# Attention and a 7x7 depthwise convolution with group norms: the second norm's statistics on ScalarE, attention steps in groups of eight, and half a convolution tile moved to VectorE

## Chip, cores and metric

The kernel runs on one core of a Trainium2 chip. The metric is device time in microseconds (us). TensorE (PE) multiplies matrices, VectorE (DVE), ScalarE (ACT) and GpSimd (POOL) work on rows of 128 partitions, and SyncE (SP) issues transfers. Every engine takes its instructions in the order in which the program lists them, and transfers are issued by SP, by GpSimd and, at the very end, by ScalarE.

## The reference

x has 16 images of 384 channels and 32 x 32 pixels, in float32. Both layers begin with a group norm over 32 groups of 12 channels (no learned scale), and both add their result to their input:

```python
x = x + attention(gn(x))     # 8 heads of 48 channels, 1x1 convolutions for q,k,v and for the output, a bias
x = x + depthwise(gn(x), w)  # 7x7, padding 3; w is the mean of the weight and its three rotations

def gn(v):                   # per image and group of 12 channels
    return (v - mean(v)) / sqrt(var(v) + 1e-5)
def attention(h):            # n = 1024 pixels are the tokens
    q, k, v = split(w_qkv @ h)
    return w_proj @ (softmax(q @ k.T / sqrt(48)) @ v) + b_proj
```

Below, x1 is the sum after the first layer: it is the input of the second norm, and the convolution is added to it.

## The kernel before

**Layout.** Channels lie on the partitions, in three tiles of 128 channels by 1024 pixels per image. The four rotations make the 49 weights of a channel, wsym. The attention of an image is cut into four units, one for each pair of heads; a unit has 16 steps, two halves of the queries by eight tiles of 128 keys. The S part of a step (L425) multiplies k with q for both heads of the pair into a PSUM tile of 128 x 1024, and ScalarE takes the exponential of it (L433). The AV part (L441) multiplies the exponentials with v and adds up over the eight key tiles; a column of ones in v gives the sum of the exponentials. After eight AV parts ScalarE copies the result, o, to SBUF (L452). The maximum is not subtracted; a check at the end repeats everything by another path if a sum was out of range.

**One image on TensorE.** S and AV parts are issued in groups: first the S parts of a group, then other work, then its AV parts, then other work. The sizes of the groups are a list:

```python
SIZES = [7] * 8 + [8]        # 64 steps of an image
```

The other work is the q,k projection of the next image in six chunks (`qk_step`, L374, evacuated at L381), the v projection in four (`v_step`, L400, L409) and the output projection in three (`proj_step`, L492). Three PSUM tiles of 128 x 1024 (ps_s) serve S and all of this in turn, and two of 128 x 512 (ps_o) serve AV.

**From o to the output projection.** `finish` sends the row of sums out and back through DRAM (two rows out, one transfer back, all by SP) so that they lie on 128 partitions; `finish2` (`invert`) takes the reciprocal on VectorE and sends it out and back, spread over 64 partitions a head; `finish3` (`divide`) multiplies. For the last unit of an image six rows of o are then copied by SP into the three packed tiles that the projection reads. `project` follows: three times a projection, evacuated on ScalarE with the bias added, and x added to the result by an accumulating transfer that GpSimd issues. The six rows that complete the packed q,k tiles (`qk_rest`) go through SP too.

**The norms.** The class `Stats` has the steps of one norm: `channels` (L230: BATCH_NORM_STATS2 on VectorE, twice a tile), `gather` (two transfers by GpSimd that bring the 12 channels of a group together), `groups` (aggregate and an inverse square root of about 14 small VectorE operations, then two transfers to spread the scales to the channels) and `apply` (L296: one ScalarE operation a tile). For the first and the last image `groups_on_pe` averages over groups with small matmuls instead. The statistics of x for images 2 to 15 are taken once, early: 42 tiles stream in (`stream_in`, `stream_stats`), `stream_groups` computes all scales, and seven transfers bring them to the tile x_sc through DRAM (gr_all, L363). `begin_x` loads x of the next image once v of the current one is done, and queues its apply.

**The convolution.** VectorE does it by taps (`conv_tap`, L549): x1 += w * shifted xn, one operation for each of the 49 offsets and each tile, up to three tiles in turn. Four of the 48 tiles (channel tiles 2 and 1 of images 14 and 15, PE_TILES) are done by TensorE instead, in pieces (`conv_on_pe`, L651; halves h = 0 and 1 of the rows, two parts each), with shifted copies of xn (sh, `conv_load`) that come from DRAM; VectorE adds the result at the end (L664). The tile (15, 0), LONE, is summed in two accumulators (`tap_of_two`), which are added at L804.

**The order.** It is written out by the program itself, which keeps two model clocks, `clock` for TensorE and `vclock` for VectorE (US_STEP 1.716 us a step, US_TURN 0.353 a group, and so on). `after(wait, cost, f)` puts a VectorE operation on a heap, due at a model time. `catch_up` issues due operations and, between them, taps, until vclock has reached clock. `applies` is a queue of ScalarE work with due times; its head is issued behind the S parts of a group. `other` issues the other work of TensorE: a due output projection, or chunks.

**The end.** In the first and the last image `fast_finish` and `fast_end` take the place of `finish` and `project`: the sums of the last unit are added up on TensorE (`divide_at_once`), the output projection is done in parts (`proj_part`), and the norm is grouped on TensorE. Behind that the loop issues TensorE's last convolution pieces, and taps beside them, until nothing is left.

## Time and profile before

| what | value |
|---|---|
| median of 3 runs | 2978.39 us (2976.01 to 2980.45) |
| profiled execution | 2982.38 us, its span 2980.2 us |
| granted TensorE clock, mean | 0.996 |
| busy: PE, DVE, ACT, POOL | 2943.7, 2626.3, 1326.4, 200.7 us |
| PE: S, AV, q,k, v, output projections, convolution | 918.4, 910.7, 509.9, 254.6, 220.0, 96.1 us |
| DVE: taps (L549), 2132 of them | 2328.0 us |
| ACT: exponentials (L433), 1024 of them | 954.4 us |
| transfers | 171.27 MB |

The median is over executions that were not profiled; the profiled execution gives all other rows. Its span is what the profile covers, and 2.2 us of its time lie outside the span. The busy time of an engine is the sum over its instructions; the groups of the page add it up by program line, and a row names the output and the inputs with their shapes. Timelines give the start and the length of runs of instructions in us from the start of the span.

### The profile page before, as it was taken

Reading aid. Unit: us, or ns where it says so; the run is one execution under the profiler, and the core shown is the slowest. Engines: PE = TensorE matmul, PEld = TensorE weight load, DVE = VectorE, ACT = ScalarE, POOL = GpSimd, SP = SyncE. Lnnn points to the kernel's source line nnn. Section 1 sums busy time; section 2 is a strip of 40 time slices with the busy share of each in tenths; the row PEclk is TensorE's granted clock in tenths of the full one; section 3 lists DMA queues with packets and bytes.
Section 4 is the critical chain, followed back from the end, with each engine's and each line's share of the span. In section 5 each row is a group of like instructions: output and inputs, shape, how many; then the busy total and the mean of one; then the engine's idle time right before and its main releaser. Section 6 shows DMA issues by size and latency. Waiting matters only on the chain.

```text
span 2980.2 us, 30719 instructions
## 1 busy us (share of the span) xinstructions
PE 2943.7 (99%) x11702; PEld 1191.2 (40%) x11702; DVE 2626.3 (88%) x2771; ACT 1326.4 (45%) x1509; POOL 200.7 (7%) x304
## 2 busy tenths in 40 slices
PE   7999999999999999999999999999999999999998
PEld 4334343343434334343433434343343433434333
DVE  0545983999999999999999999999999999999985
ACT  2533445435354544535454453544445454444600
POOL 0211300000000000000010000001000000100000
PEclk9999999999999999999999999999999999999999
DMA  2641121121312203121120312213031221312424
GB/s 74 241 135 34 24 73 30 26 63 37 66 37 53 51 15 67 43 59 45 31 72 15 67 37 54 56 26 77 16 67 37 52 51 26 67 32 45 119 74 105
DMA packets 73101, 171.27 MB, mean 57 GB/s; under 512 B 30208, under 2 KB 32624, under 8 KB 71408
## 3 DMA queue, kind: packets, MB, share of 16 engines
q0 software_dynamic: 29760, 97.89, 12.1%
q1 hardware_dynamic: 41104, 67.06, 9.9%
q10 hardware_dynamic: 2080, 4.26, 0.6%
q8 instruction: 94, 1.54, 0.2%
q14 instruction: 63, 0.52, 0.1%
HBM read 121.61 MB, written 29.46 MB: 51 GB/s over the span
## 4 chain that ended last, share of the span: by engine, by line
PE 76%; issue 11%; DMA 1%; DVE 1%; POOL 0%; ACT 0%; SPq 0%; POOLq 0%; DVEq 0%
PE ps_s L425 24%; PE acc L441 24%; PE ps_qk L374 14%; PE ps_v L400 7%; PE ps_proj L492 6%; PE ps_conv L651 1%; DVE x L549 1%; DMA x<-in_x 0%; DMA out<-x 0%; DMA sh<-xd 0%; DVE bs_x L230 0%; DMA x_sc<-gr_all 0%; DMA gr_x<-af_x 0%; DVE sum L549 0%; POOL out L559 0%
## 5 line engine op out<-in xcount | busy, mean ns | idle before, releaser
L549 DVE SCALAR_TENSOR_TENSOR x<-xn,wsym,x 128x960 f32<-128x960 f32 (+9 forms) x2132 | 2328.0, 1166 | 49.0 <-ACT xn L296 47.5
L433 ACT ACTIVATE e<-ps_s 128x1024 f32<-128x1024 f32 x1024 | 954.4, 1048 | 357.1 <-PE ps_s L425 353.4
L425 PE MATMUL ps_s<-qk 48*128 48x512 f32 x4096 | 918.4, 597 | 0.0
L441 PE MATMUL acc<-e,v 128*64 128x512 f32 x4096 | 910.7, 596 | 0.0
L425 PEld LDWEIGHTS ps_s<-qk 48*128 48x128 f32 x4096 | 380.0, 185 | 534.4 <-issue 240.6
L441 PEld LDWEIGHTS acc<-e,v 128*64 128x64 f32 x4096 | 281.1, 137 | 608.5 <-issue 600.5
L374 PE MATMUL ps_qk<-x,wqk 128*128 128x512 f32 x1152 | 509.9, 599 | 6.1 <-ACT x L296 3.7
L374 PEld LDWEIGHTS ps_qk<-x,wqk 128*128 128x128 f32 x1152 | 216.4, 191 | 297.2 <-issue 266.4
L381 ACT COPY qk<-ps_qk 128x1024 f32<-128x1024 f32 x96 | 97.2, 1012 | 444.1 <-PE ps_qk L374 444.1
L400 PE MATMUL ps_v<-wv,x 128*128 128x384 f32 x768 | 254.6, 492 | 0.0
L452 ACT COPY o<-acc 128x512 f32<-128x512 f32 x128 | 76.0, 594 | 337.9 <-PE acc L441 337.9
L492 PE MATMUL ps_proj<-o,wp 128*128 128x512 f32 x504 | 220.0, 595 | 0.0
L400 PEld LDWEIGHTS ps_v<-wv,x 128*128 128x128 f32 x768 | 146.0, 192 | 110.3 <-ACT e L433 11.4
L492 PEld LDWEIGHTS ps_proj<-o,wp 128*128 128x128 f32 x504 | 94.6, 190 | 124.5 <-issue 111.2
L409 ACT COPY v<-ps_v 128x384 f32<-128x384 f32 x128 | 55.1, 483 | 187.8 <-PE ps_v L400 187.8
L153 POOL DMA_DIRECT2D x<-in_x x45 | 24.0, 539 | 1536.7 <-ACT v L409 1535.2
L319 DVE BATCH_NORM_STATS2 bs_all<-xs 128x6 f32<-128x512 f32 x84 | 52.5, 680 | 83.8 <-DMA xs<-in_x 83.7
L500 ACT ACTIVATE x<-ps_proj,bp 128x1024 f32<-128x1024 f32 x42 | 46.8, 1113 | 167.7 <-PE ps_proj L492 159.7
L230 DVE BATCH_NORM_STATS2 bs_x<-x 128x6 f32<-128x512 f32 x108 | 69.0, 684 | 50.5 <-DMA x<-in_x 40.9
L477 DVE TENSOR_TENSOR o<-o,inv 128x1024 f32<-128x1024 f32 x62 | 75.5, 1217 | 33.0 <-DMA inv<-inv 22.6
L651 PE MATMUL ps_conv<-sh,mat 128*32 128x480 f32 (+3 forms) x896 | 96.1, 587 | 2.5 <-DMA sh<-xd 2.5
L501 POOL DMA_DIRECT2D x<-in_x x42 | 36.5, 870 | 468.7 <-ACT x L500 463.6
(92 smaller groups left out, 516.1 us busy)
## 6 DMA issues: line engine op xcount, KB each, us to landing
x<-in_x POOLq DMA_DIRECT2D x93, 512.0 KB, 5.4
inv<-inv SPq DMA_DIRECT2D x124, 256.0 KB
out<-x POOLq DMA_DIRECT2D x48, 512.0 KB, 3.7
xs<-in_x POOLq DMA_DIRECT2D x42, 512.0 KB, 6.1
qk<-qk SPq DMA_DIRECT2D x96, 128.0 KB
sh<-xd SPq DMA_DIRECT2D x38, 160.0 KB
o<-o SPq DMA_DIRECT2D x84, 64.0 KB
sh<-xd ACTq DMA_DIRECT2D x26, 160.0 KB
```

Source lines behind the costliest of these rows:

```text
L230: nc.vector.bn_stats(self.bs[:, k, 6 * h : 6 * h + 6], src[:, h * HALF : (h + 1) * HALF])
L374: nc.tensor.matmul(ps[:, h, :], lhsT=wqk[:, k, s, t, :], rhs=xns[b][:, k, h * HALF : (h + 1) * HALF], start=(k == 0), stop=(k == NK - 1),)
L381: nc.scalar.copy(halves(qks[u][:, s, :]), ps)
L400: nc.tensor.matmul(ps[:, j, 0:C], lhsT=xns[b][:, k, t * P : (t + 1) * P], rhs=wv[:, k, :], start=(k == 0), stop=(k == NK - 1),)
L425: nc.tensor.matmul(ps[:, j, :], lhsT=qks[u][r, 1, i * P : (i + 1) * P], rhs=qks[u][r, 0, h * HALF : (h + 1) * HALF], start=True, stop=True,)
L433: nc.scalar.activation(es[n], ps, AF.Exp, scale=SCALE)
L441: nc.tensor.matmul(accs[u, h][64 * j : 64 * j + 64, :], lhsT=v_of(u, i, j), rhs=e[:, j, :], start=(i == 0), stop=(i == NT - 1),)
L452: nc.scalar.copy(os_[u][:, h * HALF : (h + 1) * HALF], accs.pop((u, h)))
L477: nc.vector.tensor_tensor(os_[u], os_[u], invs.pop(u), ALU.mult)
L492: nc.tensor.matmul(ps[:, h, :], lhsT=wp[:, t, o * P : (o + 1) * P], rhs=os_[NP * b + t][:, h * HALF : (h + 1) * HALF], start=(t == 0), sto ...
L549: nc.vector.scalar_tensor_tensor(acc, xn1s[b, k].rearrange("p (h w) -> p h w", w=W)[:, iy, ix], wsym[:, k, dy + PAD, dx + PAD : dx + PAD + 1],
L651: nc.tensor.matmul(pss[b, k][CH * i : CH * (i + 1), h, :].rearrange("p (y x) -> p y x", x=W)[:, :, ox], lhsT=mats[k][:, i, d0 * KS + dx + ...
```

## The change

The change has five parts.

- **Groups.** An image has eight groups of eight steps. Thresholds that name a step of the image (r) are set to multiples of eight.
- **Statistics of x1, images 1 to 12.** The evacuation of the output projection on ScalarE also accumulates its sum over the pixels (`psums`); with the mean of x, kept from the statistics of x (`x_mean`), that gives the mean of x1 (`x1_means`, one VectorE operation). Three squares on ScalarE, with accumulated outputs, give the variances (`square`). The layout is that of the bn statistics, with one entry of six numbers a channel in place of two, so that `gather_x1` moves half as much and VectorE aggregates in one operation. The inverse square root is ln, exp and a product on ScalarE (`groups_x1`). Images 13 and 14 keep VectorE's statistics.
- **Places.** ScalarE's queue `applies` now holds a cost for each entry, and `act_slot(free)` issues entries, behind the S parts of a group or ahead of a q,k chunk, as long as they fit into the time given. The apply of the next image's x goes between the first two and the third output projection (`pending`), or behind the S parts of a group in the images after 0 and 15. For the last unit of an image the waits of `finish` are 6 and 5.5 us instead of 9 and 9.5, and the projection is due 7 us after the division, not 8.
- **Half a tile.** Of the tile (14, 1), SHARED, TensorE does the lower half of the rows only (h = 1); the taps of the upper half go to VectorE. TensorE has 14 pieces of convolution at the end in place of 16.
- **The end.** Taps are issued between the steps of `fast_finish` and `groups_on_pe`, VectorE's model clock gets 4 us behind `fast_finish` in place of 3, and the lone tile takes turns with the others.

The diff, cut to its core:

```diff
 xns, x1s, qks, os_, accs, es, xn1s = {}, {}, {}, {}, {}, {}, {}
-xds, shs, pss, mats = {}, {}, {}, {}
+xds, shs, pss, mats, psums = {}, {}, {}, {}, {}
...
 PE_TILES = [(b, k) for b in (B - 2, B - 1) for k in PE_K]
+SHARED = None if general else (B - 2, PE_K[1])
...
         inverse_sigma(af.unsqueeze(1), mv[:, 0:1], mv[:, 1:2], self.name)
+        self.spread(af)
+    def spread(self, af):
...
         )
-    def groups_on_pe(self, masks):
+    def square(self, src, k):
+        t = tpool.tile([P, N], F32, tag="t", name=f"sq_{self.name}_{k}")
+        nc.scalar.activation(
+            t, src, AF.Square, bias=self.bs[:, k, 1:2], accum_out=self.bs[:, k, 2:3]
+        )
+    def gather_x1(self):
+        ch_d = ddram.tile([C, 6], F32, tag="ch1", name=f"ch_{self.name}")
+        nc.gpsimd.dma_start(ch_d.rearrange("(k p) s -> p k s", p=P), self.bs)
+        self.gs = small.tile([GROUPS, PER * 6], F32, tag="gs1", name=f"gs_{self.name}")
+        nc.gpsimd.dma_start(self.gs, ch_d.rearrange("(g e) s -> g (e s)", e=PER))
+    def aggregate(self):
+        self.mv = small.tile([GROUPS, 2], F32, tag="mv", name=f"mv_{self.name}")
+        nc.vector.bn_aggr(self.mv, self.gs)
+    def groups_x1(self):
+        af = small.tile([GROUPS, 2], F32, tag="af", name=f"af_{self.name}")
+        ln = small.tile([GROUPS, 1], F32, tag="ln", name=f"ln_{self.name}")
+        nc.scalar.activation(ln, self.mv[:, 1:2], AF.Ln, bias=eps[0:GROUPS])
+        nc.scalar.activation(af[:, 0:1], ln, AF.Exp, scale=-0.5)
+        nc.scalar.activation(
+            af[:, 1:2], self.mv[:, 0:1], AF.Identity, scale=af[:, 0:1]
+        )
+        self.spread(af)
+    def groups_on_pe(self, masks, between=lambda: None):
...
         average(0, mean)
+        between()
...
         average(NK, d)
+        between()
...
         )
+def means_of(bs, dst):
+    nc.vector.tensor_reduce(dst, bs[..., 1::3], AX.X, ALU.add)
+    nc.vector.tensor_scalar(dst, dst, -0.25, None, ALU.mult)
...
     M = B - 2
+    means_of(many["bs"], x_mean[:, 2:, :])
...
 def proj_step(b, o):
     ps = psum(f"ps_proj_{b}_{o}")
+    if o == 0:
+        psums[b] = small.tile([P, NK], F32, tag="psums", name=f"psums_{b}")
...
     x1s[b, o] = rpool.tile([P, N], F32, tag="x1", name=f"x1_{b}_{o}")
-    nc.scalar.activation(halves(x1s[b, o]), ps, AF.Identity, bias=bp[:, o : o + 1])
+    nc.scalar.activation(
+        halves(x1s[b, o]),
+        ps,
+        AF.Identity,
+        bias=bp[:, o : o + 1],
+        accum_out=psums[b][:, o : o + 1],
+    )
...
 def conv_tap(b, k, dy, dx, dst=None):
     (oy, iy), (ox, ix) = region(dy, dx)
+    if (b, k) == SHARED:
+        oy = slice(oy.start, min(oy.stop, H // 2))
+        iy = slice(iy.start, oy.stop - oy.start + iy.start)
...
 def conv_end(b, k):
+    if (b, k) == SHARED and not late.get("shared"):
+        late["shared"] = True
+        return
...
 def conv_on_pe(b, k, h, part):
-    if (h, part) == (0, 0):
+    if (b, k) not in pss:
...
 def conv_on_pe_end(b, k):
-    nc.vector.tensor_tensor(
-        halves(x1s[b, k]), pss.pop((b, k)), halves(x1s[b, k]), ALU.add
-    )
+    h = slice((b, k) == SHARED, 2)
+    dst = halves(x1s[b, k])[:, h]
+    nc.vector.tensor_tensor(dst, pss.pop((b, k))[:, h], dst, ALU.add)
...
 NS = U * 2 * NT
-SIZES = [7] * 8 + [8]
+SIZES = [8] * 8
...
 def us_tap(dy, dx):
     late_us = 0.02 if clock > last_image else 0.0
-    return ((H - abs(dy)) * (W - abs(dx)) + (128 if len(active) > 1 else 268)) / 955 + late_us
+    rows = H - abs(dy)
+    if tuple(active[0][0:2]) == SHARED:
+        rows = H // 2 - max(0, -dy)
+    return (rows * (W - abs(dx)) + (128 if len(active) > 1 else 268)) / 955 + late_us
...
 def tap():
...
         return 0.0
-    if active[0][0:2] == [*LONE] and len(active) > 1:
-        active.append(active.pop(0))
...
     if (b, k) == LONE:
-        return tap_of_two(b, k, active[0])
+        active.append(active.pop(0))
+        return tap_of_two(b, k, active[-1])
...
 x1_stats = {}
-pe_conv, pe_loads = deque(), deque((bk, h, a) for bk in PE_TILES for h in range(2) for a in range(2))
+pe_conv, pe_loads = deque(), deque((bk, h, a) for bk in PE_TILES for h in range(bk == SHARED, 2) for a in range(2))
...
 lims = []
-applies = deque()
+applies, pending = deque(), []
+ON_VECTOR = (B - 3, B - 2)
...
 def project(b):
...
         clock += US_PROJ
-        after(8.0, 1.3, lambda o=o: x1_part(b, o))
+        if b in ON_VECTOR:
+            after(8.0, 1.3, lambda o=o: x1_part(b, o))
+        if o == 1 and pending:
+            pending.pop()()
+    if b not in ON_VECTOR:
+        after(1.6, 0.2, lambda: x1_means(b))
...
 def x1_part(b, k):
...
         st.gather()
-        after(7.0, 3.3, lambda: x1_groups(b, st))
+        after(6.0, 3.3, lambda: x1_vector_groups(b, st))
+def x1_vector_groups(b, st):
+    st.groups()
+    applies.append((now() + 7.5, 3.7, lambda: x1_chains(b, st)))
+def x1_means(b):
+    st = x1_stats[b] = Stats(f"x1_{b}")
+    st.bs = x1_bs[:, b % 2]
+    nc.vector.scalar_tensor_tensor(
+        st.bs[:, :, 1::3],
+        psums.pop(b).unsqueeze(2).to_broadcast([P, NK, 2]),
+        -1.0 / N,
+        x_mean[:, b, :].unsqueeze(2).to_broadcast([P, NK, 2]),
+        ALU.mult,
+        ALU.add,
+    )
+    applies.append((now() + 4.5, 4.2, lambda: x1_squares(b, st)))
+def x1_squares(b, st):
+    for k in range(NK):
+        st.square(x1s[b, k], k)
+    st.gather_x1()
+    after(11.0, 0.6, lambda: x1_aggregate(b, st))
+def x1_aggregate(b, st):
+    st.aggregate()
+    applies.append((now() + 0.5, 0.6, lambda: x1_groups(b, st)))
 def x1_groups(b, st):
-    st.groups()
-    applies.append((now() + 10.0, lambda: x1_chains(b, st)))
+    st.groups_x1()
+    applies.append((clock + 8.0, 3.7, lambda: x1_chains(b, st)))
+def act_slot(free):
+    while applies and applies[0][0] <= clock and applies[0][1] <= free:
+        _, cost, f = applies.popleft()
+        free -= cost
+        f()
...
             conv_store(b, k)
-            pe_conv.extend((b, k, h, part) for h in range(2) for part in range(2))
+            pe_conv.extend(
+                (b, k, h, part)
+                for h in range((b, k) == SHARED, 2)
+                for part in range(2)
+            )
...
         0.0,
-        lambda: chains.extend((b, k) for k in range(NK) if (b, k) not in on_pe),
+        lambda: chains.extend(
+            (b, k) for k in range(NK) if (b, k) not in on_pe or (b, k) == SHARED
+        ),
...
     else:
-        applies.append((now() + 14.0, lambda: x_apply(b, None)))
+        pending.append(lambda: x_apply(b, None))
...
         st.channels(xns[b][:, k, :], k)
+    means_of(st.bs, x_mean[:, b, :])
...
     st.groups()
-    applies.append((now() + 12.0, lambda: x_apply(b, st)))
+    applies.append((now() + 12.0, 3.7, lambda: x_apply(b, st)))
...
 def finish(u):
...
         waiting.add(u)
-        after(9.0, 0.3, lambda: finish2(u))
+        after(6.0 if u % NP == NP - 1 else 9.0, 0.3, lambda: finish2(u))
...
 def finish2(u):
     invert(u)
-    after(9.5, 1.3, lambda: finish3(u))
+    after(5.5 if u % NP == NP - 1 else 9.5, 1.3, lambda: finish3(u))
...
 def finish3(u):
...
     if p == NP - 1:
-        proj.append((now() + 8.0, b))
+        proj.append((now() + 7.0, b))
...
 def other(done):
...
     credit = min(credit + 0.45, 2.0)
+    catch_up(clock)
...
                 break
+            if kind == "qk" and i % 2 == 0:
+                act_slot(4.5)
...
 def fast_finish(b):
...
     proj_part(b, 0, (NP - 2,))
+    tap(), tap()
...
     x1_stats[b] = Stats(f"x1_{b}")
+    tap(), tap()
...
     clock += 2 * US_PROJ + 1.0
-    vclock = clock + 3.0
+    vclock = clock + 4.0
 def fast_end(b):
-    x1_stats[b].groups_on_pe(late["masks"])
+    x1_stats[b].groups_on_pe(late["masks"], tap)
...
     else:
-        if applies and applies[0][0] <= clock:
-            applies.popleft()[1]()
+        if r and pending and b - 1 in FAST:
+            applies.append((clock, 3.7, pending.pop()))
+        catch_up(clock)
+        act_slot(4.5)
...
     if b == B - 1:
-        if once("mat_0", r >= 14):
+        if once("mat_0", r >= 16):
...
             late["w3"] = mat[:, 2 * SH * KS * CH :][:, 0:C]
-        if once("w", r >= 28 and b - 1 in x1_stats):
+        if once("w", r >= 32 and b - 1 in x1_stats):
...
             nc.sync.dma_start(late["w3"], w4[:, NK])
-        if once("mat_1", r >= 21):
+        if once("mat_1", r >= 24):
             conv_matrices(1, flat2(qkpool.tile([P, 2, N], F32, tag="qk", name="mat_1")))
-        if once("ones", r >= 28):
+        if once("ones", r >= 32):
...
     if b in FAST:
-        if r >= 35 and (b, 0) not in x1s and all(c[0] > b - 2 for c in active):
+        if r >= 32 and (b, 0) not in x1s and all(c[0] > b - 2 for c in active):
...
                 )
-    if b == B - 1 and r in (35, 42, 49):
+    if b == B - 1 and r in (32, 40, 48):
...
```

## The prediction, made before the changed kernel ran

> **What bounds the kernel now.** I read the page's busy shares first, then TensorE's timeline in a steady image, then the chain of work that ended last around 300 us, then VectorE's timeline at the end.
>
> ```profile
> PE 2943.7 (99%) x11702; PEld 1191.2 (40%) x11702; DVE 2626.3 (88%) x2771; ACT 1326.4 (45%) x1509; POOL 200.7 (7%) x304
> ...
> L549 DVE SCALAR_TENSOR_TENSOR x<-xn,wsym,x 128x960 f32<-128x960 f32 (+9 forms) x2132 | 2328.0, 1166 | 49.0 <-ACT xn L296 47.5
> ```
>
> TensorE is busy 99% of the span; VectorE's taps wait 47.5 us for ScalarE's xn, once an image: VectorE is not what the middle waits for. What shortens the run must take work or idle time from TensorE, or shorten what follows its last big stage.
>
> TensorE's timeline, one group of eight steps and one of seven (start, us, instruction; S is ps_s, AV is acc):
>
> ```profile
> 2507.76 7.14 PE L425 MATMUL ps_s<-qk 48*128 48x512 f32 x32
> 2514.83 7.09 PE L441 MATMUL acc<-e,v 128*64 128x512 f32 x32
> 2521.85 6.28 PE L425 MATMUL ps_s<-qk 48*128 48x512 f32 x28
> ...
> 2577.91 6.28 PE L425 MATMUL ps_s<-qk 48*128 48x512 f32 x28
> 2584.12 6.23 PE L441 MATMUL acc<-e,v 128*64 128x512 f32 x28
> 2590.28 10.57 PE L374 MATMUL ps_qk<-x,wqk 128*128 128x512 f32 x24
> ```
>
> From start to start, eight steps take 14.09 us and seven 12.37, with no gap. The one large stall in the middle is early; the chain (start, us, what):
>
> ```profile
> 276.58 20.03 issue
> 296.62 0.04 POOLq L363
> 296.66 0.50 issue
> 297.16 3.79 DMA x_sc<-gr_all
> 300.95 0.02 issue
> 300.97 1.25 ACT x L296
> 302.22 0.04 issue
> 302.26 12.26 PE ps_qk L374 x24
> ```
>
> The scales of images 2 to 15 (x_sc) are fetched once. They arrive at 300.95, ScalarE applies them to x, and the q,k projection of image 2, which TensorE reached at 298.51, starts at 302.26. The end, on VectorE:
>
> ```profile
> 2877.18 5.58 DVE L549 SCALAR_TENSOR_TENSOR x<-xn,wsym,x 128x899 f32<-128x899 f32 x4
> ...
> 2942.84 1.23 DVE L804 TENSOR_TENSOR x<-x,sum 128x1024 f32<-128x1024 f32 x1
> ...
> 2967.74 1.23 DVE L664 TENSOR_TENSOR x<-ps_conv,x 128x1024 f32<-128x1024 f32 x1 [21.66 <-PE ps_conv L651]
> ```
>
> VectorE has finished its own tiles at 2944.07 and waits 21.66 us for TensorE's convolution: TensorE sets the end, and VectorE has that much room there.
>
> **What the Trainium skill says.** "TensorE: Matmul & The Clock Gate", What's actually happening: after about 3.4 us of idleness TensorE runs at half rate for a while. The trace agrees: after the 3.75 us stall 24 matmuls took 12.26 us, elsewhere 10.50. "ScalarE: Activation LUTs", What ACT_TABLE_LOAD costs: 1283 ns a load and 1380 ns of drain. The trace has one load, 1283 ns; no row shows the drain. The same page, Table sets, says one set holds both ln and exp. The built program nevertheless has a load ahead of each ln and another ahead of each exp: 24 in all.
>
> **The change, part by part.**
>
> *Groups of eight.* An image had eight groups of seven and one of eight: 8 x 12.37 + 14.09 = 113.05 us. Now 8 x 14.09 = 112.72. Sixteen images: **5.3 us off TensorE**.
>
> *The scales of image 2.* The same grouping, and the new slot for image 2's apply, put its q,k projection behind 16 steps of image 1 instead of 21; the built order shows S, V, AV, S, AV, qk. What feeds it is unmoved: GpSimd issues af_all and gr_all behind the x loads, which wait for image 1's V, then come 20 us for gr_all and 4 for x_sc. V ends 0.5 us later (one more S step, 0.86, less 0.33), so the scales come at 301.5 and the projection starts at 302.8. TensorE gets there at 268.0 (V) + 7.0 + 14.1 = 289.1. It waits 13.7 us where it waited 3.75: **9.9 us lost**. The slow clock afterwards is paid in both. Behind this apply on ScalarE stand a copy of o and later exps; TensorE waits anyway.
> The first such place, image 1's apply in image 0, also moves earlier: TensorE is there at 127.4, not 132.9. Before, the scales (130.45) waited for two stream tiles that GpSimd issued behind the statistics' transfers; now 18 tiles, not 16, stand ahead of those. I count 88.7 for VectorE's first tile, 17.9 for 14 tiles, 3.6 for x, 0.5 for the new means, 4.9 for four tiles, 3.1 for the group arithmetic, 6.8 for two transfers: 125.5, first x tile at 126.8. No stall, 0.6 us of room; if the tiles are as late as before, 5.6 us.
>
> *Statistics of x1 on ScalarE* (images 1 to 12). VectorE loses six BATCH_NORM_STATS2 (0.64 each by their starts) and 14 small operations, about 6 us an image; it gains one small operation and, on SP and GpSimd, nothing (two of four small transfers halve). As VectorE waits for xn in every image, that is worth nothing to the end. ScalarE gains three squares, priced as three xn applies (3.5 us), and ln, exp, identity with two loads. Its room is the AV phase: exps trail S by 1.4 us, AV lasts 7.0, and the copy of o may slip 0.5: 6.1 us. Squares fit. The ln slot costs 2 x 1.28 + 3 x 0.2 = 3.2 by the trace's load, 2 x 2.66 + 0.75 = 6.1 by the page's price: it fits, barely at the top. Behind ln stand a copy of o and the next eight exps, for which S waits. Taken: 0.05 us an image, 0.6 in all; ends 0 (nothing speeds up: TensorE was not waiting) and 25 (2 us each). Accumulated outputs lengthen evacuations that have three PSUM buffers behind them: nothing.
>
> *Projection earlier.* It now follows V directly, 22.8 us after the last AV of the previous image instead of 34. What it needs, by image 2's rows: copy of o 0.7, two small transfers to 4.5, reciprocal; SP is issuing six qk rows until 6.5 and their packets run to 9.1, so the reciprocal leaves at 10.4 and is back at 15; divide 1.2; the first o rows land at about 20, the last at 23, of which the first matmuls need two and the last ones 3.4 us later the rest. Room 2.7 us: nothing. VectorE idles some 5 us more an image there, within its 13 us of room. Image b+1's x lands at 29, its apply between projections comes at 34.
>
> *Half a conv tile.* 16 pieces of TensorE become 14. After the stall for sh, 779 records of 56 a piece ran from 2885.85 to 2967.6: 5.88 us a piece, **11.8 us off TensorE's tail**. VectorE gains 49 half taps. Taps of 841 and 992 elements start 1.00 and 1.16 us apart; a half tap has 458 on average: 0.60 us, 29 us in all. Of these the built order leaves 11 behind the last image's xn, and 11 whole taps of tile (14,0) where 5 were. Before, that stretch took 2944.07 - 2877.18 = 66.9 us, 1.36 of it waiting for TensorE's check. Now 65.5 + 6 x 1.07 + 11 x 0.60 + 0.7 (adds) = 79.2, and the check, reached at 30.6 with TensorE there at 32.9, adds 2.3: 81.5. TensorE ends at 90.4 - 11.8 = 78.6. The last add, at 90.6 before, starts at 81.5: **9.1 us gained, not 11.8; VectorE now sets the end**. Two output transfers leave together: 0.5 us.
>
> *Taps in the end's waits.* The waits are 1.22, 2.92, 1.82, 3.04 us; one or two taps go in each (0.6 to 1.7), and the chain resumes with TensorE's conv piece, unmoved. VectorE, coming to the last image's first reciprocal perhaps 1.5 us late, may push this by 0.5 (0 to 2).
>
> Sum: -5.3 + 9.9 + 0.6 - 9.1 + 0.5 + 0.5 = -2.9. The profiled execution took 2982.4 (2980.2 span, 2.2 around it): 2979.5. It lies 4 above the median of the runs, 2978.4; from that, 2975.5.
>
> **Rivals.**
> 1. *ScalarE's ln slot holds up TensorE* (slower). In every second image VectorE's mv is due about 77 us into the image and the slot opens at 78.4. If loads cost the page's price, the 6.1 us are full, and each us that mv or a load is late stops exp, then S. It decides from 0.1 us over; 1.5 us in each of 12 images gives 18: 2993. For: an in-order queue with no spare time. Against: the trace's load is half that price.
> 2. *The early projection waits for o* (slower). Were the rows 3.7 us later than counted, 14 images would lose 1 us each: 2989. For: in the early, crowded stretch the reciprocal's return took 9.17 us longer than VectorE. Against: the traffic of an image's turn is known row by row.
> 3. *The early stall does not grow* (faster). If gr_all's 20 us were queueing behind the x loads rather than its own small elements, the scales would come as much sooner as the order allows: -2.9 - 9.9, 2966. Against: x's packets need 5.3 us, not 20.
> 4. *Nothing of it reaches the end*: the tail keeps TensorE's length because VectorE takes more than 90.6: +6, 2984.
>
> **How the numbers follow.** 0.2% of the median is 6 us, about what a measurement of this kernel can tell from no change. Chances: the forecast 0.52 (its own range 2969 to 2983), rival 1 0.13, rival 2 0.10, rival 3 0.17, rival 4 0.08. Of the forecast 0.10 lies below 2972.4 and 0.03 above 2984.4. Faster: 0.17 + 0.10 = 0.27; slower: 0.13 + 0.09 of rival 2 + 0.03 + half of rival 4 = 0.29; the same 0.44. The range reaches to rival 3 and into rivals 1 and 2: 2966 to 2990.
>
> **What would show it.** In the profile after: TensorE idle about 13.7 us before image 2's q,k projection; 14.09 us a group; no idle at the projections or after the ln slots; VectorE's last add waiting less than 1 us for TensorE instead of 21.66, with the final stretch 81 us long; ScalarE some 85 us busier. A TensorE gap in each image, or the last add still waiting for ps_conv, proves me wrong.

## The result, and the profile after

The changed kernel takes 2975.46 us (median of 6 runs, 2973.1 to 2978.29), the kernel before 2978.09 us in its runs beside it (6 runs). The ratio is 0.9991, with a 95% interval of 0.9978 to 1.0004: no difference that this measurement can tell. The forecast was 2975.5 us, with "the same" as the likeliest case. The profiled execution took 2978.29 us (span 2976.5), which is 2.8 above the median of its kernel, as that of before was above its own. Two profiles can therefore differ by a few us where the medians do not; below, medians compare kernels, and profiles tell where time lies. "The changed kernel" is the kernel after.

The page after, busy time by engine and the taps' group (out<-in, count, busy us, mean ns, idle time before and what ended it):

```profile
PE 2926.9 (98%) x11590; PEld 1185.5 (40%) x11590; DVE 2580.1 (87%) x2596; ACT 1414.6 (48%) x1683; POOL 198.7 (7%) x307
L607 DVE SCALAR_TENSOR_TENSOR x<-xn,wsym,x 128x899 f32<-128x899 f32 (+11 forms) x2181 | 2351.0, 1149 | 29.7 <-ACT xn L338 29.7
```

TensorE is 16.8 us less busy, ScalarE 88 us more (85 were expected), VectorE 46 us less although it has 49 taps more. TensorE's share fell from 99 to 98%: it lost work and gained idle time. Where the idle time is, TensorE's timeline shows (start, us, instruction, and in brackets the idle time before it and what ended it):

```profile
120.80 7.09 PE L488 MATMUL acc<-e,v 128*64 128x512 f32 x32
130.47 11.98 PE L421 MATMUL ps_qk<-x,wqk 128*128 128x512 f32 x24 [2.59 <-ACT x L338]
...
286.83 7.09 PE L488 MATMUL acc<-e,v 128*64 128x512 f32 x32
307.12 12.40 PE L421 MATMUL ps_qk<-x,wqk 128*128 128x512 f32 x24 [13.20 <-ACT x L338]
```

And ScalarE's, at the same places:

```profile
129.18 3.50 ACT L338 ACTIVATE x<-x,sc_x 128x1024 f32<-128x1024 f32 x3 [6.78 <-DMA sc_x<-gr_x]
...
305.83 3.51 ACT L338 ACTIVATE x<-x,x_sc 128x1024 f32<-128x1024 f32 x3 [17.36 <-DMA x_sc<-gr_all]
```

Image 2's q,k projection waits 13.20 us where it waited 3.75: TensorE is there at 293.92, the scales only at 305.83. Image 1's waits 2.59 us; in the kernel before it followed its AV part without a gap:

```profile
126.74 6.23 PE L441 MATMUL acc<-e,v 128*64 128x512 f32 x28
132.90 10.57 PE L374 MATMUL ps_qk<-x,wqk 128*128 128x512 f32 x24
```

Behind both waits of the changed kernel 24 matmuls take 12.0 to 12.4 us instead of 10.5. In a steady image there is no gap, as in this stretch of image 8:

```profile
1483.98 15.75 PE L447 MATMUL ps_v<-wv,x 128*128 128x384 f32 x48
1499.56 15.61 PE L541 MATMUL ps_proj<-o,wp 128*128 128x512 f32 x36
1515.11 7.09 PE L488 MATMUL acc<-e,v 128*64 128x512 f32 x32
1522.12 10.57 PE L421 MATMUL ps_qk<-x,wqk 128*128 128x512 f32 x24
1532.62 7.14 PE L472 MATMUL ps_s<-qk 48*128 48x512 f32 x32
```

The projection begins at once behind V. From V to V an image takes 175.33 us (mean of images 3 to 15), before 175.87. ScalarE's slot with ln and exp lies in this image at 1555:

```profile
1547.88 7.44 ACT L480 ACTIVATE e<-ps_s 128x1024 f32<-128x1024 f32 x8 [0.47 <-PE ps_s L472]
1555.34 1.28 ACT L288 ACT_TABLE_LOAD   x1
1556.63 0.29 ACT L288 ACTIVATE ln_x<-mv_x,eps 32x1 f32<-32x1 f32 x1
1556.95 1.28 ACT L289 ACT_TABLE_LOAD   x1
1558.24 0.20 ACT L289 ACTIVATE af_x<-ln_x 32x1 f32<-32x1 f32 x1
1558.47 0.29 ACT L290 ACTIVATE af_x<-mv_x,af_x 32x1 f32<-32x1 f32 x1
1560.91 0.59 ACT L499 COPY o<-acc 128x512 f32<-128x512 f32 x1 [2.14 <-PE acc L488]
```

It takes 3.43 us from 1555.34 on, and 2.14 us are left ahead of the copy of o. The end, on VectorE:

```profile
2884.84 4.76 DVE L607 SCALAR_TENSOR_TENSOR x<-xn,wsym,x 128x960 f32<-128x960 f32 x4
...
2961.43 1.08 DVE L607 SCALAR_TENSOR_TENSOR x<-xn,wsym,x 128x841 f32<-128x841 f32 x1
2962.54 1.23 DVE L867 TENSOR_TENSOR x<-x,sum 128x1024 f32<-128x1024 f32 x1
2963.68 1.22 DVE L727 TENSOR_TENSOR x<-ps_conv,x 128x1024 f32<-128x1024 f32 x1
```

There is no bracket at the last add: VectorE no longer waits for TensorE, whose last convolution matmul ended at 2960.62. VectorE sets the end.

### The profile page after: what moved, and what is told of

It reads as the page before. It is cut to its first block, busy times and chain, and to the rows that moved or that the text cites. A ratio compares the mean times of both kernels' runs of the same rounds, so it can differ in the third digit from the quotient of the medians.

```text
span 2976.5 us, 30347 instructions
## 1 busy us (share of the span) xinstructions
PE 2926.9 (98%) x11590; PEld 1185.5 (40%) x11590; DVE 2580.1 (87%) x2596; ACT 1414.6 (48%) x1683; POOL 198.7 (7%) x307
## 4 chain that ended last, share of the span: by engine, by line
## 5 line engine op out<-in xcount | busy, mean ns | idle before, releaser
L607 DVE SCALAR_TENSOR_TENSOR x<-xn,wsym,x 128x899 f32<-128x899 f32 (+11 forms) x2181 | 2351.0, 1149 | 29.7 <-ACT xn L338 29.7
L155 POOL DMA_DIRECT2D x<-in_x x45 | 24.1, 543 | 1503.8 <-PE ps_v L447 1308.1
L712 PE MATMUL ps_conv<-sh,mat 128*32 128x464 f32 (+3 forms) x784 | 83.9, 584 | 0.0
L338 ACT ACTIVATE xn<-x,sc_x 128x1024 f32<-128x1024 f32 x44 | 52.1, 1284 | 28.6 <-DVE sc_x L328 28.5
L338 ACT ACTIVATE x<-x,x_sc 128x1024 f32<-128x1024 f32 x42 | 48.9, 1229 | 17.4 <-DMA x_sc<-gr_all 17.4
```

Of the source, the lines that this page charges most:

```text
L338: nc.scalar.activation(dst, src, AF.Identity, bias=self.sc[:, k, 1:2], scale=self.sc[:, k, 0:1],)
L607: nc.vector.scalar_tensor_tensor(acc, xn1s[b, k].rearrange("p (h w) -> p h w", w=W)[:, iy, ix], wsym[:, k, dy + PAD, dx + PAD : dx + PAD + 1],
L712: nc.tensor.matmul(pss[b, k][CH * i : CH * (i + 1), h, :].rearrange("p (y x) -> p y x", x=W)[:, :, ox], lhsT=mats[k][:, i, d0 * KS + dx + ...
```

## The experiments

Each kernel ran beside the kernel before, whose median in these runs was 2977.0 to 2977.5 us. An edit is against the changed kernel where nothing else is said. "Theory" in the quoted expectations is what the prediction and the two traces suggested; "the planner" is the part of the program that writes out the order.

The changed kernel did not run beside the experiments. A difference of medians to it is known to 4 to 6 us only, by the intervals of the two ratios to the kernel before. Part of that is scatter early in an execution. The kernels without the half tile, with the old place of the projection, with image 12's or all statistics moved, with the statistics on VectorE and without taps in the waits issue the same instructions as the changed kernel up to image 2's q,k projection. In their profiles the step behind it starts at 313.5 to 316.3 us, in that of the changed kernel at 319.45. So each profile is cut in two below, at the first matmul that adds up sums of the last image (ps_sum). What follows, up to the start of VectorE's last add, is called the tail.

| kernel | ps_sum starts at (us) | tail (us) |
|---|---|---|
| before | 2835.11 | 132.63 |
| changed | 2841.01 | 122.67 |
| groups of eight alone | 2838.38 | 129.37 |
| half tile back on TensorE | 2835.44 | 128.90 |
| projection at its old place | 2837.60 | 152.15 |
| one image's statistics late | 2837.32 | 134.17 |
| all statistics early | 2835.08 | 120.17 |
| statistics on VectorE | 2835.92 | 119.77 |
| no taps in the waits | 2837.81 | 126.08 |
| ln and exp three times | 2902.05 | 121.93 |
| early applies later | 2841.67 | 135.16 |
| early order | 2833.73 | 121.02 |
| early order, with the wait in the plan | 2826.13 | 119.82 |

### Groups of eight alone

```diff
 (the kernel before)
-            SIZES = [7] * 8 + [8]
+            SIZES = [8] * 8
...
```

The thresholds that name a step (r) change with it.

> The kernel before with groups of eight alone (and the thresholds on a step of the image that go with them); nothing else of the change. Theory: eight groups save 5.3 us on TensorE, but the q,k projections of images 1 and 2 come earlier than their scales: image 2's wait grows from 3.75 to 13-14 us, image 1's from 0 to 2.5-4.5 us plus 1.4 us of slow clock behind it. Sum -5.3 + 9.7 + 5 = +9 us against the kernel before, about 2987 us (2983 to 2990). Rival: the early waits belong to the change's other parts (the new places of the applies) and groups of eight alone have none: -5 us, about 2973 us.

Measured: 2984.37 us, 1.0030 (1.0018 to 1.0042), so +6.9 us against the kernel before, at the lower edge of what the theory gave. Its TensorE timeline has the early waits without any other part of the change:

```profile
129.03 10.57 PE L374 MATMUL ps_qk<-x,wqk 128*128 128x512 f32 x24 [2.50 <-ACT x L296]
...
282.29 7.09 PE L441 MATMUL acc<-e,v 128*64 128x512 f32 x32
301.26 12.39 PE L374 MATMUL ps_qk<-x,wqk 128*128 128x512 f32 x24 [11.88 <-ACT x L296]
```

By the medians the regrouping alone is a loss: it saves 5.3 us in 16 images and brings TensorE too early to two places. The profiles do not show that loss; that is taken up under what stays open.

### The half tile back on TensorE

```diff
-            SHARED = None if general else (B - 2, PE_K[1])
+            SHARED = None
```

> The changed kernel with the whole tile (14, 1) back on TensorE: 16 pieces instead of 14. Theory: TensorE's convolution then ends 11.8 us later, at about 2972.4 us of the span instead of 2960.6, and the last add of VectorE, which started at 2963.7, waits for it: +8.7 us, less 0.4 since two outputs do not leave together, about 2983.5 us (2982 to 2985). Rival: the half tile brought nothing, the tail is set by the norm of the last image and its transfers: within 2 us of the changed kernel, 2975.5 us.

Measured: 2979.79 us, 4.3 us more than the changed kernel where 8.0 were expected, and below the range given. The tail, free of the early scatter, is 6.2 us longer (128.90 for 122.67). VectorE's last lines show the wait for TensorE back in full:

```profile
2936.31 1.23 DVE L867 TENSOR_TENSOR x<-x,sum 128x1024 f32<-128x1024 f32 x1
2941.47 1.22 DVE L727 TENSOR_TENSOR x<-ps_conv,x 128x1024 f32<-128x1024 f32 x1 [3.94 <-PE ps_conv L712]
2964.34 1.23 DVE L727 TENSOR_TENSOR x<-ps_conv,x 128x1024 f32<-128x1024 f32 x1 [21.64 <-PE ps_conv L712]
```

So TensorE's end does decide without the half tile, but it came sooner than expected: from ps_sum on TensorE's convolution ends 9.2 us later than in the changed kernel, not 11.8. TensorE's pieces, from start to start, tell part of why. Steady pieces take 5.71 us in every kernel, 0.17 less than the 5.88 a piece of the prediction, which include the slow stretch behind the wait for sh; the third piece, which waits for sh, took 10.57 us in the kernel before, 6.94 here and 7.32 with groups of eight alone. Some 3.3 us of the tail's gain over the kernel before thus come with the groups of eight, whose thresholds move the first loads of sh to steps 32, 40 and 48: with the groups alone the tail is 3.3 us shorter (129.37 for 132.63). Besides, TensorE begins the convolution 1.1 us sooner here, since VectorE with fewer taps is in time for the last image's division.

### The projection at its old place

```diff
-                    after(6.0 if u % NP == NP - 1 else 9.0, 0.3, lambda: finish2(u))
+                    after(9.0, 0.3, lambda: finish2(u))
-                after(5.5 if u % NP == NP - 1 else 9.5, 1.3, lambda: finish3(u))
+                after(9.5, 1.3, lambda: finish3(u))
-                    proj.append((now() + 7.0, b))
+                    proj.append((now() + 8.0, b))
```

> The changed kernel with the waits of the last unit as before (9 and 9.5 us, the projection due 8 us after the division); the projection then follows the AV parts of the group instead of V directly. Theory: in the changed kernel V and the projection are neighbours on TensorE, and V and the projection took 0.10 us less each (15.58 for 15.68, 15.54 for 15.65); that is lost again in 13 images: +2.7 us, about 2978 us (2975 to 2980), with no wait at the projections in either. Rival: the early projection costs a hidden wait for rows of o, and without it the kernel is faster, 2972 us or less.

Measured: 3004.71 us, 29 us more than the changed kernel: both theories missed. TensorE behaves as expected (V and projection 15.68 and 15.65 us again, 175.51 us an image, no wait) and ends at 2955.05. VectorE is the late one: the tail is 29.5 us longer. ScalarE's xn of image 12, first in the changed kernel and then in this one, and VectorE's last operation in this one:

```profile
2431.64 3.55 ACT L338 ACTIVATE xn<-x,sc_x 128x1024 f32<-128x1024 f32 x3
```

```profile
2466.62 3.55 ACT L338 ACTIVATE xn<-x,sc_x 128x1024 f32<-128x1024 f32 x3
```

```profile
2989.75 1.23 DVE L867 TENSOR_TENSOR x<-x,sum 128x1024 f32<-128x1024 f32 x1
```

The xn comes 35 us later. Counted from the V ahead of it, the projection of image 12 starts 7.1 us later than in the changed kernel, the squares 32.7 and the xn 38.9: squares, ln and xn go into three of ScalarE's slots, a group or more apart, and with the later projection the squares miss slots that they had, so that xn stands at step 40 of the image instead of 24 or 32. VectorE stands idle for xn 89.6 us in all (29.7 in the changed kernel), and 107 taps are left behind the last image's xn instead of 71. The early projection, priced at nothing in the prediction, is what lets ScalarE's three slots come early enough.

### One image's statistics late

```diff
-                applies.append((now() + 4.5, 4.2, lambda: x1_squares(b, st)))
+                applies.append((now() + (18.0 if b == B - 4 else 4.5), 4.2, lambda: x1_squares(b, st)))
```

> The changed kernel with the squares of image 12 alone one group later (due 18 us after the means): its xn comes at step 32 instead of 24. Theory: what a late xn costs is paid at the end, because VectorE's room in the middle is not room there: VectorE's order leaves 9 taps more (5 half ones, 4 whole ones) behind the last xn, +7.3 us, about 2982.8 us (2980.5 to 2985), with TensorE as before. Rival: VectorE waits for xn in every image, so 14 us in one image are absorbed: within 2 us of the changed kernel, 2975.5 us.

Measured: 2984.59 us, +9.1 against the changed kernel. One xn, of the fourth image from the end, comes a group (14.09 us) later, and the tail is 11.5 us longer. Behind the last xn VectorE has 80 taps instead of 71, and takes 7.5 us more. The other 4.0 us lie ahead of it: VectorE, in arrears, comes late to the last image's division, and TensorE's last projection waits for it, where the changed kernel waits 1.00 us:

```profile
2865.86 6.25 PE L579 MATMUL ps_proj<-o,mat 128*128 128x512 f32 x10 [3.04 <-DVE o L571]
```

### All statistics early

```diff
-                applies.append((now() + 4.5, 4.2, lambda: x1_squares(b, st)))
+                applies.append((now() + 2.5, 4.2, lambda: x1_squares(b, st)))
```

> The changed kernel with one number changed: the squares of x1 are due 2.5 us after the means instead of 4.5, so that from image 2 on every image has its squares, its ln and its xn at steps 8, 16 and 24, where the changed kernel has every second image one group (14 us) later. Theory: VectorE's order then leaves 20 taps of image 14 behind the last xn instead of 22, and VectorE sets the end: -1.7 us, about 2973.8 us (2972 to 2975). Rival: squares so early wait for x1's accumulating transfers and hold up the exponentials: TensorE waits at image after image, 2985 us or more.

Measured: 2970.08 us, 0.9979 (0.9972 to 0.9986) of the kernel before, 5.4 us less than the changed kernel and more than the 1.7 expected. In the changed kernel xn stands at step 24 in one image and at step 32 in the next. With all of them at 24 the order leaves two taps fewer at the end, and VectorE, less in arrears, also brings TensorE's last convolution on 0.3 us sooner. In the tail that is 2.5 us. The two profiles differ by 8.4 us in all, and 5.9 of that is there at 320 us already: a later start, image 1's wait (1.72 us with no slow clock behind it, 2.59 with one) and image 2's (11.78 for 13.20). On ScalarE and VectorE the two kernels' instructions are the same up to 826 us, so these 5.9 us are scatter and not the edit. What the edit itself gives is thus 2.5 us; the rest of the medians' 5.4 is not shown to come from it. No wait for x1's transfers appeared.

### The statistics back on VectorE

```diff
-            ON_VECTOR = (B - 3, B - 2)
+            ON_VECTOR = tuple(range(1, B - 1))
```

> The changed kernel with x1's statistics of images 1 to 12 back on VectorE (as images 13 and 14 have them); groups, half tile, early projection and taps in the waits stay. Every xn then comes at step 24, and 68 taps stand behind the last xn instead of 71. Theory: what the statistics are worth is when xn comes, not VectorE's 6 us an image: 3 taps less, as early as the kernel with squares due after 2.5 us: about 2971 us (2968.5 to 2974). Rival: VectorE's 72 us of work have to go somewhere, and the end gets a part of them: 2980 us or more.

Measured: 2969.89 us, as forecast and equal to the kernel with the squares early (2970.08). Its tail is 119.77 us, that of the other 120.17. VectorE's 69 us more of busy time (2649.4) cost nothing: every xn comes at step 24, and 68 taps stand behind the last one. ScalarE's statistics bring nothing by themselves; what matters is when they are ready.

### Taps out of the end's waits

```diff
-                tap(), tap()
-                tap(), tap()
-                vclock = clock + 4.0
+                vclock = clock + 3.0
-                x1_stats[b].groups_on_pe(late["masks"], tap)
+                x1_stats[b].groups_on_pe(late["masks"])
```

> The changed kernel without taps in the end's waits (and the 4 us back to 3). 77 taps then stand behind the last xn instead of 71. Theory: six taps, three of them half ones, are 5.0 us at the end; VectorE comes to the last image's reciprocal and sums about 1 us earlier: +4 us, about 2979.5 us (2977 to 2982). Rival: the taps in the waits delay the chain of the last norm by as much as they take: 2975.5 us within 2 us.

Measured: 2976.68 us, 1.2 more than the changed kernel, within the scatter. The tail is 3.4 us longer, close to the 4 expected, and shows both halves of the trade. From the first tap behind the last xn to the last add VectorE takes 5.2 us more, and that first tap comes 1.8 us sooner after V of the last image.

### ln and exp three times

```diff
+                    for _ in range(3):
-                    nc.scalar.activation(ln, self.mv[:, 1:2], AF.Ln, bias=eps[0:GROUPS])
-                    nc.scalar.activation(af[:, 0:1], ln, AF.Exp, scale=-0.5)
+                        nc.scalar.activation(ln, self.mv[:, 1:2], AF.Ln, bias=eps[0:GROUPS])
+                        nc.scalar.activation(af[:, 0:1], ln, AF.Exp, scale=-0.5)
```

> The changed kernel with ln and exp of the group norm done three times over (the same values), so that ScalarE's slot takes 3.43 + 2 x 3.08 = 9.6 us instead of 3.43. Theory: the slot's room is 6.1 us (2.1 us were left behind ln, exp and the product, plus what exponentials may slip); 3.5 us too many stop the copy of o and the exponentials behind it, and S with them: 12 images by 2.5 to 3.5 us, +30 to +42 us, about 3011 us (3003 to 3018). Rival: PSUM and SBUF buffers ahead of AV absorb it: within 3 us of the changed kernel, 2975.5 us.

Measured: 3039.58 us, +64 us: the mechanism, at twice the expected price. TensorE, in one of the twelve images:

```profile
670.60 2.85 PE L473 MATMUL ps_s<-qk 48*128 48x512 f32 x12
676.25 6.30 PE L473 MATMUL ps_s<-qk 48*128 48x512 f32 x20 [2.81 <-ACT e L481]
682.48 7.09 PE L489 MATMUL acc<-e,v 128*64 128x512 f32 x32
```

The gap is 2.81 us, as worked out, but the S parts take 11.88 us from start to start instead of 7.07. Of the 4.81 us lost, 1.8 lie in the 20 matmuls behind the gap. All twelve gaps are 2.80 or 2.81 us long; behind six of them the 20 matmuls take 6.30 us, as here, behind the others 7.3 to 7.7. From V to V the loss is 5.6 us an image. The window of that place (from and to, length, then busy us of PE, PEld, DVE, ACT and POOL with their instructions, the granted TensorE clock, DMA share, GB/s) shows a halved clock:

```profile
678.00:680.00 2.00, 2.00 (x6) 0.98 (x6) 2.00 (x3) 1.87 (x3) 0.72 (x1) 0.50 0.00 0
```

### The early applies a group later

```diff
-                applies.append((now() + 12.0, 3.7, lambda: x_apply(b, st)))
+                applies.append((now() + 18.0, 3.7, lambda: x_apply(b, st)))
-                    if r and pending and b - 1 in FAST:
+                    if r >= 24 and pending and b - 1 in FAST:
```

> The changed kernel with the two early applies a group or two later (image 1's due 18 us after its groups instead of 12; image 2's from step 24 of image 1 on), so that TensorE does S and AV parts while the scales are under way. Theory: the early waits are a matter of order and not of work, and go: 13.2 (image 2) + 1.9 (its slow clock) + 2.6 + 1.4 (image 1) = 19.1 us less than the changed kernel, about 2956.5 us (2954 to 2960). Rival: the six q,k chunks then stand too close together in what is left of image 1, or the wait turns up at the next place: half of it or less is gained, 2966 us or more.

Measured: 2987.77 us, 12 us more than the changed kernel: the rival's case, and worse. The early waits shrank to 2.74 us, and a new one appeared at the projection of image 1. The two places on TensorE:

```profile
319.05 10.57 PE L421 MATMUL ps_qk<-x,wqk 128*128 128x512 f32 x24 [2.74 <-ACT x L338]
...
445.36 15.23 PE L541 MATMUL ps_proj<-o,wp 128*128 128x512 f32 x28 [15.66 <-DMA o<-o]
```

So nothing was gained early: ps_sum starts 0.7 us later than in the changed kernel. The loss is in the tail, 12.5 us longer: the planner's slots changed places, and image 12 was among those with xn at step 32 (80 taps behind the last xn).

### The early order, with chunks spaced closer

A q,k chunk is issued once `credit`, which grows at every visit of `other`, is large enough.

```diff
-                applies.append((now() + 4.5, 4.2, lambda: x1_squares(b, st)))
+                applies.append((now() + 2.5, 4.2, lambda: x1_squares(b, st)))
-                credit = min(credit + 0.45, 2.0)
+                credit = min(credit + (0.7 if b == 1 else 0.45), 2.0)
-                    if r and pending and b - 1 in FAST:
+                    if r >= 16 and pending and b - 1 in FAST:
```

> The previous edit (squares due after 2.5 us), and image 2's x applied from step 16 of image 1 on instead of step 8, with the q,k chunks of that one image spaced closer (credit 0.7 a visit instead of 0.45), so that the last chunk still lies two groups ahead of the next image. Theory: TensorE does S and AV parts while the scales arrive; image 2's wait of about 12.5 us and its slow clock of 1.9 go, and since no q,k rows stand in SP's queue ahead of the reciprocal the wait does not turn up at the projection, as it did when the chunks stayed late: -14.4 - 1.7, about 2959.5 us (2956 to 2963). Rival: the wait only moves on (another projection, VectorE at the end): 2970 us or more.

Measured: 2969.84 us, no better than the kernel with the squares early alone. V of image 2 starts at 412.45, in the kernel with the squares early alone at 426.12, so the early wait is gone; 9.80 us of it are back at the projection. The chain of waits tells from what (start, us, what):

```profile
398.63 24.50 DVE x L607 x23
423.14 0.17 DVE rec L513
423.31 0.02 issue
423.33 1.40 DMA inv<-rec
...
425.28 3.91 DMA inv<-inv
...
431.39 6.48 DMA o<-o
437.86 0.14 issue
438.00 7.23 PE ps_proj L541 x11
```

The copy of o was done at 406.1, but 23 taps stand ahead of the reciprocal in VectorE's queue, and it starts at 423.14. VectorE is behind its plan: earlier it waited 15.36 us for GpSimd in the group arithmetic of images 2 to 15 (af_all), to which the planner gives 3.6 us. In the changed kernel the same reciprocal starts later still, at 428.83, and TensorE, held up by its early wait, loses nothing by it.

### The same, with VectorE's wait in the plan

```diff
 (the kernel of the last experiment)
-            after(4.0 * len(every) + 34.0, 3.6, stream_groups)
+            after(4.0 * len(every) + 34.0, 34.0, stream_groups)
```

> The early order again (squares due after 2.5 us, image 2's x applied from step 16 on, q,k chunks of image 1 closer), and the planner's cost of the group arithmetic of images 2 to 15 raised from 3.6 to 34 us, which is nearer to what VectorE spends there waiting for GpSimd (15.4 us): 14 taps fewer stand ahead of the last reciprocal of image 1. Theory: in the early order the projection of image 1 waited 9.8 us since VectorE came to that reciprocal 12 us late, at 423.05 us where the sums were there at about 411; with 14 taps (15 us) less ahead of it the wait goes, and the slow clock behind it: 2969.8 - 11.7, about 2958 us (2955.5 to 2961.5). Rival: the wait is that of the transfers of o, or VectorE pays the taps back at the end: 2967 us or more.

Measured: 2955.90 us, 0.9928 (0.9915 to 0.9942) of the kernel before. TensorE, from image 1's last S and AV parts ahead of the q,k projection to the output projection, has no bracket left:

```profile
301.03 7.09 PE L488 MATMUL acc<-e,v 128*64 128x512 f32 x32
308.04 10.57 PE L421 MATMUL ps_qk<-x,wqk 128*128 128x512 f32 x24
...
417.04 15.75 PE L447 MATMUL ps_v<-wv,x 128*128 128x384 f32 x48
432.63 7.89 PE L541 MATMUL ps_proj<-o,wp 128*128 128x512 f32 x18
```

VectorE now waits for the sums, instead of the sums for VectorE:

```profile
413.83 0.25 DVE L513 RECIPROCAL rec<-sums 128x16 f32<-128x16 f32 x1 [0.68 <-DMA sums<-sum]
```

It is the fastest of all kernels here, 19.6 us below the changed one, far outside the scatter. Its own end is balanced: TensorE's convolution ends at 2944.12, VectorE's last add starts at 2945.95. The 34 us that the planner now allows are more than the 15.4 of waiting and the 3.6 of work together; no value between was tried.

## Why the prediction was right, and where it was not

**The sum** was forecast at -2.9 us against the profiled execution; its span moved by -3.7. Up to ps_sum of the last image the profile is 5.9 us longer than that of before (forecast 5.2 with the statistics' 0.6), the tail is 10.0 shorter (forecast 9.1, less 0.5 for the taps in the waits), and 0.4 us more follow the last add (forecast 0.5). The two large terms have the right sign and nearly the right size, and they cancel as forecast. That the sum came so close is in part luck: 4.0 us at image 1 were missed on one side, 0.21 us an image and 1.4 us of the tail on the other, and the scatter between executions is larger than the sum.

**Groups of eight** were right: 14.09 us a group. But an image became 0.54 us shorter, not 0.33. The other 0.21 was missed: V and the output projection are now neighbours and take 15.58 and 15.54 us instead of 15.68 and 15.65. The kernel with the projection at its old place gives most of it back (175.51 us an image).

**The scales of image 2** were right: a wait of 13.20 us for 13.7, put down to the grouping by the kernel that has the grouping alone. The prediction's third rival, that gr_all's 20 us would shorten, did not occur: from V's end to the first apply it is 33.3 us, before 33.4. What it did not see is how little of the wait could be had by better order alone: VectorE, late by then, was the next to be waited for.

**The scales of image 1** were wrong. The step said that they come at 125.5 and TensorE at 127.4, "no stall". TensorE was in time (127.88), the scales were used at 129.18. With the slow clock behind the 2.59 us this cost 4.0 us in this execution, within the 5.6 left open there. In the profiles of most other kernels the wait was 1.72 to 2.66 us, and no slow clock followed.

**The statistics on ScalarE** cost TensorE nothing: 0.6 us was taken, the slot is 3.43 us long by the trace where 3.2 was counted, and no TensorE gap follows it. The Trainium skill's "ScalarE: Activation LUTs", What ACT_TABLE_LOAD costs, adds 1380 ns of drain to a load of 1283. Here the load took 1283 ns and the next ACTIVATE began 10 ns behind it (1555.34 + 1.28, then 1556.63), so the low end of the range, which I had taken, was right. Rival 1 was real as a mechanism, as the tripled pairs show, but its point of decision seems to lie further out than 6.1 us: at 9.6 us of slot TensorE waited 2.8, so by estimate about 6.8 us are free.

**The step that failed** is "As VectorE waits for xn in every image, that is worth nothing to the end", and the same reasoning in "VectorE idles some 5 us more an image there, within its 13 us of room". Work that VectorE does not have while it waits, it does later, and the taps slip toward the last image: 9.1 us for one group's delay in image 12, 29 us for the old place of the projection. The page's sum of the waits for xn does not tell this: with all statistics early it is 59.2 us, in the changed kernel 29.7, and yet two taps fewer are left at the end. The sum came out right nevertheless because the number of taps behind the last xn had been read off the built order, in which those delays are already contained.

**The tail** was forecast to gain 9.1 us at the last add. From the first tap behind the last xn to the last add VectorE took 78.8 us, forecast 81.5. Most of the difference is the 2.3 us of waiting for TensorE's check, which did not occur: TensorE was there 29.0 us in, not 32.9, because sh no longer kept it waiting. VectorE sets the end, as forecast. The attribution was off: of the 10.0 us by which the tail is shorter, the half tile is worth 6.2 (4.3 by the medians), and 3.3 come with the groups of eight and their earlier loads of sh, which the prediction did not count. **Taps in the waits** were forecast at a 0.5 us delay of the chain (0 to 2); VectorE's first tap behind the last xn comes 1.8 us later after ps_sum than before, 1.00 of it a wait of TensorE ahead of the last projection.

**What stays open.** Groups alone cost 6.9 us by the medians (interval 5.4 to 12.5 us), and the traces do not show it: the spans of the two profiles are equal, 2980.2 us. That of groups alone is the fastest of its six runs, that of before lay above its median. In these profiles ps_sum starts 3.3 us later (-5.3 for the groups, +8.1 and +2.5 for the two waits, some 2 us less at the start and at V of image 1), and the tail is 3.3 us shorter. A slow clock behind image 1's wait, absent in this execution, would be 1.4 us of the rest. Image 1's wait of 2.8 us remains in the fastest kernel. In the kernel with the later apply of image 2 it was gone, since image 1's apply was moved too, but there VectorE waited 32.55 us for the gathered statistics (gs_all); whether the one can be had without the other was not tried.

## What to carry to other kernels

Idle time of an engine is room only if it may be filled with work that is already there. If the engine idles because its input comes late, and its backlog ends the program, then a delay of that input is paid for at the end, here with two thirds or more of it, however idle the engine looks on the page.

When a reordering exposes a wait, look at which engines are late at that moment before removing it. Here TensorE's 13 us of wait covered a VectorE that was nearly as late, and the wait only moved until the planner allowed for VectorE's own wait (15 us for GpSimd).

## What the runs showed of the hardware that was not expected

- A TensorE gap of 2.81 us cost 4.81. Behind the gap of 2.59 us at image 1 the granted clock was 0.50 from 130.4 to 133.0. The Trainium skill's "TensorE: Matmul & The Clock Gate", What's actually happening, gives an idle window of about 3.4 us before the clock is halved; here gaps shorter than that were followed by a halved clock too, but not all of them. Behind the twelve gaps of 2.80 and 2.81 us in the kernel with three pairs, and behind 2.81 us in the fastest kernel, matmuls were slow; behind 1.72 to 2.66 us at image 1 in nine other kernels, and behind the 2.74 us with the later applies, 24 matmuls took 10.57 us, as with no gap. So a wait on TensorE can cost more than its length in the chain, here by 1.4 to 3.2 us or by nothing, and two executions with nearly the same wait can differ by that.
- An accumulated output is an instruction of its own on ScalarE, 0.19 us for a projection's evacuation and 0.22 us for a square (78 of them, 16.2 us of busy time in all). It overlaps its neighbours: between two squares of image 12 the second starts 0.10 us after it.
